# Selective scan on Trainium2: who adds the carried state, and how a product is cut between two engines

## The chip, the cores and the metric

The kernel runs on one core of one Trainium2 chip. The metric is the device time of one execution in microseconds (us); the time of the kernel before is the median of three runs. A core has five engines that run side by side, each with its own queue that is worked off in order: TensorE (PE, matrix products; its weight loads are shown as PEld), VectorE (DVE), ScalarE (ACT), GpSimd (POOL) and SyncE (SP), which here only starts DMA transfers. Engines wait for each other through semaphores. SBUF is the working memory of 128 partitions; PSUM is a smaller memory that TensorE writes to.

## The reference, cut to what matters

Four layers work on two images of 128 channels and 64 x 64 pixels: an attention layer, a layer of deformable convolutions, a residual convolution layer, and a selective scan ("Mamba") that reads each normalised image in four directions. Only the fourth is changed. Its core, for one direction of one image, with L = 4096 pixels, 256 inner channels and N = 16 states for each channel:

```python
dt = jax.nn.softplus(dt @ W_dt.T + b_dt)
A = -jnp.exp(A_log)
dA = jnp.exp(dt[..., None] * A)
dBu = dt[..., None] * Bm[:, :, None, :] * xh[..., None]

def step(h, inp):
    dA_t, dBu_t = inp
    h = dA_t * h + dBu_t
    return (h, h)
h0 = jnp.zeros((Bn, d_inner, N), x.dtype)
_, hs = lax.scan(step, h0, (dA.transpose(1, 0, 2, 3), dBu.transpose(1, 0, 2, 3)))
y = jnp.einsum('lbdn,bln->bld', hs, Cm)
```

So each of 256 x 16 sequences has a decay `dA`, an input `dBu` and a state `h` that runs through all 4096 pixels. The state starts from zero at the head of a direction.

## The kernel before, in words

The first three layers, which the change doesn't touch, fill the first 2450 us. The fourth, `layer3` (from L1121), has a short head and then, from about 2500 us to the end, one long loop (L1630).

**Tiling.** A direction is cut into 8 blocks of 512 pixels (`BLK`), so that two images of four directions make 64 blocks. In a block the 256 channels are two halves (`hf`) and the 16 states are four sets of four (`ng`): 8 groups `k`, in the order hf 0 with ng 0 to 3, then hf 1. A group covers 128 channels x 4 states; it is laid out as 4 scans (`q`, 32 channels each) of 128 partitions (4 states x 32 channels) and 512 columns. Every block therefore has 32 scans. Directions that run backwards read the same tiles from the last column to the first (`reverse`).

**What a group needs.** Six steps on four engines:

- *Input product* `dBu`, tile `db` (128 x 4 x 512): B times (dt times x), for all four scans. VectorE makes it in `db_dve` (L1413), with B spread over partitions by TensorE into a PSUM tile `pbc`; GpSimd makes it in `db_pool` (L1422), with B spread by DMA into an SBUF tile `b`. The table `ND` (L1130) says how many of the four scans are VectorE's: all four for five groups of a block, none for two (hf 0 ng 1 and hf 1 ng 2), and one of four for hf 0 ng 2, the mixed group.
- *Decay* `da` (128 x 512, PSUM): one exponential for each scan on ScalarE, `expo` (L1430).
- *Scan*: VectorE, `scan` (L1439), which runs h = da * h + db along the columns and overwrites `db`. Its start is the constant 0.0 in the first block of a direction, and else the column of `hl` that belongs to this group and scan.
- *Last state*: ScalarE, `keep` (L1444), which copies the last column of the group's four scans to `hl`, for the same group of the next block.
- *Product with C*: GpSimd, `cmul` (L1449), in place, after `keep`, since it overwrites the states.
- *Sum over states*: TensorE, `sums` (L1457).

**Order.** The loop writes the order of every engine's queue by hand (`manual_schedule`), group by group (k) and scan by scan (q). ScalarE makes decays two scans ahead (`AHEAD`), and the PSUM pool holds three `da` tiles, so that the decay of a scan waits until the scan three before it has ended. VectorE's product of group k+1 follows the last scan of group k; GpSimd's product of group k+2 follows `cmul(k-1)`. Between the groups, `front_act` gives ScalarE the next block's preparation: copies behind L1319's product (L1325, L1327), softplus, and two silu steps with table loads (L1300, L1313). In 13 of the 64 blocks the next image's normalisation runs as well (`ln_mean` to `ln_store`), one step to a slot.

The lines around the change:

```python
                for q in range(4):
                    ...
                    if 4 * k + q + AHEAD < len(units):
                        expo(*units[4 * k + q + AHEAD])
                    ...
                    if q == 0 and ended:
                        keep(k - 1)
                    if live:
                        scan(k, q)
```

Of the kernel before, what the change touches and what calls it, by code (L numbers as in the profile page):

```python
# [15 lines left out]
AF = mybir.ActivationFunctionType  # L16
ALU = mybir.AluOpType
# [3 lines left out]
P = 128  # L21
# [3 lines left out]
BLK = 512  # L25
NBLK = L // BLK
# [1094 lines left out]
def layer3(g, I, out):  # L1121
# [5 lines left out]
    nc, tc = g.nc, g.tc  # L1127
    NJ = 4

    ND = ((4, 0, 1, 4), (4, 4, 0, 4))  # L1130
    NNG = N_STATE // NJ
    HB = 1
    HC = 3
    with ExitStack() as ctx:
# [41 lines left out]
        d4 = ctx.enter_context(tc.tile_pool(name="l3d4", bufs=2))  # L1176
# [25 lines left out]
        hl = a.tile([P, 2, NNG, 4, 1], F32, name="hl")  # L1202
# [34 lines left out]
        def ln_log(b, k):  # L1237
            nc.scalar.activation(N[k, "sq"], N[k, "var"], AF.Ln, bias=g.eps5)
# [37 lines left out]
        def reverse(i):  # L1276
            b, nd, _ = blocks[i]
            return dirs[b][nd][2]

        S = {}  # L1280
# [113 lines left out]

        def copies(i, x, ng):

            if x == "b" and ND[0][ng] == ND[1][ng] == 4:
                return
            t = S[i][x, ng] = ck.tile([P, BLK], F32, name=f"{x}4_{ng}", bufs=1)
            r0 = NJ * ng + (N_STATE if x == "c" else 0)  # L1400
            for j in range(NJ):
                nc.sync.dma_start(t[32 * j : 32 * j + 32], S[i]["bx"][r0 + j].partition_broadcast(32))

        def db_tile(k):
            if "db" not in G[k]:
                G[k]["db"] = wk.tile([P, 4, BLK], F32, name="db")
            return G[k]["db"]

        def db_dve(k):
            i, hf, ng = groups[k]  # L1410
            n = ND[hf][ng]
            if n:
                nc.vector.tensor_tensor(  # L1413
                    db_tile(k)[:, :n, :], G[k].pop("pb").unsqueeze(1).to_broadcast([P, n, BLK]),
                    S[i]["d4", hf][:, 1, :n, :], ALU.mult,
                )

        def db_pool(k):
            i, hf, ng = groups[k]
            n = ND[hf][ng]  # L1420
            if n < 4:
                nc.gpsimd.tensor_tensor(  # L1422
                    db_tile(k)[:, n:, :], S[i]["b", ng].unsqueeze(1).to_broadcast([P, 4 - n, BLK]),
                    S[i]["d4", hf][:, 1, n:, :], ALU.mult,
                )

        def expo(k, q):
            i, hf, ng = groups[k]
            da = psd.tile([P, BLK], F32, name="da")
            nc.scalar.activation(da, S[i]["d4", hf][:, 0, q, :], AF.Exp, scale=am[:, hf, q, ng : ng + 1])  # L1430
            G[k]["da", q] = da

        def scan(k, q):
            i, hf, ng = groups[k]
            d0, d1 = G[k].pop(("da", q)), G[k]["db"][:, q, :]
            if reverse(i):
                d0, d1 = d0[:, ::-1], d1[:, ::-1]
            first = i % NBLK == 0
            nc.vector.tensor_tensor_scan(d1, d0, d1, 0.0 if first else hl[:, hf, ng, q, :], ALU.mult, ALU.add)  # L1439

        def keep(k):
            i, hf, ng = groups[k]
            last = 0 if reverse(i) else BLK - 1
            nc.scalar.copy(hl[:, hf, ng], G[k]["db"][:, :, last : last + 1])  # L1444
# [46 lines left out]
        G = {}  # L1491
# [75 lines left out]
        with tc.manual_schedule():  # L1567
            tc.keep_in_program_order(nc.scalar.preload_act_table_set("natural_log_exp_and_others"))
            nc.scalar.activation(am, am, AF.Exp)
            nc.vector.tensor_scalar(am, am, -1.0, None, ALU.mult)  # L1570
            nc.vector.memset(xt[:, :HC], 0.0)
            nc.vector.memset(xt[:, HC + L :], 0.0)
            nc.vector.memset(xn[:, HB - 1, HW - HC :], 0.0)
            nc.vector.memset(xn[:, HB + HW, :HC], 0.0)
            units = [(k, q) for k in range(len(groups)) for q in range(4)]
            AHEAD = 2

            for k in range(NFIRST):
                ln_mean(0, k)
            for k in range(NFIRST):  # L1580
                ln_less(0, k)
            ln_square(0, 0)
            ln_var(0, 0)
            ln_square(0, 1)
            ln_log(0, 0)
            ln_root(0, 0)
            ln_scale(0, 0)
            ln_var(0, 1)
            ln_square(0, 2)
            ln_store(0, 0)  # L1590
            ln_var(0, 2)
            begin(0)
            conv(0, 1)
            for part in (ln_log, ln_root, ln_scale):
                for k in (1, 2):
                    part(0, k)
            conv_silu(0)
            front_pe(0, 0)
            ln_store(0, 1)
            front_act(0, 0)  # L1600
            bc_store(0)
            front_pe(0, 1)
            front_act(0, 1)
            ln_store(0, 2)
            sum_parts(0, 0)
            sum_copy(0, 0)
            spread(0, 0)
            spread_store(0, 0)
            spread_load(0, 0)
            softplus(0, 1)  # L1610
            front_pe(0, 3)
            front_act(0, 3)
            spread(0, 1)
            spread_store(0, 1)
            for ng in range(NNG):
                copies(0, "b", ng)
                copies(0, "c", ng)
            for k in range(2):
                weights(k)
            db_dve(0)  # L1620
            db_pool(0)
            front_pe(0, 4)
            front_act(0, 4)
            front_pe(0, 5)
            front_pe(0, 6)
            for u in range(AHEAD):
                expo(*units[u])
            front_act(0, 7)
            db_pool(1)
            for k in range(len(groups) + 7):  # L1630
                i, slot = divmod(k, 8)
                live = k < len(groups)
                more = k + 1 < len(groups)
                ended = 1 <= k <= len(groups)
                transfers(i + 1, slot)
                if k + 2 < len(groups):
                    weights(k + 2)
                norm = next_norm(i)
                for q in range(4):
                    if slot == 6 and q == 3 and 1 <= i <= NBK:  # L1640
                        finish(i - 1)
                    if norm and slot == 2 and q == 3:
                        ln_log(*norm)
                    if 4 * k + q + AHEAD < len(units):
                        expo(*units[4 * k + q + AHEAD])
                    if norm and q == 0:
                        if slot == 0:
                            ln_mean(*norm)
                        elif slot == 2:
                            ln_var(*norm)  # L1650
                    if q == 0 and ended:
                        keep(k - 1)
                    if live:
                        scan(k, q)

                    for j, hf in (((k - 6) // 8, 0), ((k - 10) // 8, 1)):
                        if q == 1 and 8 * j + 6 + 4 * hf == k and 0 <= j < NBK:
                            gate(j, hf)
                if norm and slot == 0:
                    ln_less(*norm)  # L1660
                if more:
                    db_dve(k + 1)
                if ended:
                    cmul(k - 1)
                if k + 2 < len(groups):
                    db_pool(k + 2)

                if slot == 5 and 0 <= k - 2 < len(groups):
                    sums(k - 2)
                if slot == 5 and 1 <= i <= NBK:  # L1670
                    project(i - 1)
                front_pe(i + 1, slot)
                front_act(i + 1, slot)
                front_pool(i + 1, slot)
                if norm:
                    if slot == 1:
                        ln_square(*norm)
                    elif slot == 3:
                        ln_root(*norm)
                    elif slot == 5:  # L1680
                        ln_scale(*norm)
                    elif slot == 6:
                        ln_store(*norm)
                if live:

                    if slot == 6 and 0 < i % (4 * NBLK) <= NBLK // 2:
                        for n in range(2):
                            turn(blocks[i][0], 2 * (i % (4 * NBLK) - 1) + n)

                if slot != 5 and 0 <= k - 2 < len(groups):  # L1690
                    sums(k - 2)
# [160 lines left out]
```

## Time and profile before

| what | value |
|---|---|
| median of three runs | 5816.95 us (5814.35 to 5819.41) |
| the profiled execution's own time | 5815.21 us |
| its span in the profile | 5813.4 us |
| VectorE busy, whole span | 4427.0 us, 76% |
| GpSimd busy, whole span | 3620.8 us, 62% |
| ScalarE busy, whole span | 3827.3 us, 66% |
| 2500 to 5798 us (the scan loop): DVE, ACT, POOL busy | 3250.7, 2455.1, 3260.2 us of 3298 |
| mean granted TensorE clock | 0.889 |

How to read it: the profile is one execution, and every time in it counts from the first instruction. A group's row names the line, the engine, the operation, what it writes and reads, and the count; after the bar come its busy time in us and the mean length of one in ns, then the idle time of its engine just before such instructions, and who ended it. Records of one engine may overlap by some tens of ns[...]; so a run of equal instructions is read by the distance of their starts. In a list in order of time, neighbours of one kind are merged into a line: start, length of the whole, and `x4` for four of them.

### The profile page before, as it was taken

Reading aid. Unit: us, or ns where it says so; the run is one execution under the profiler, and the core shown is the slowest. Engines: PE = TensorE matmul, PEld = TensorE weight load, DVE = VectorE, ACT = ScalarE, POOL = GpSimd, SP = SyncE. Lnnn points to the kernel's source line nnn. Section 1 sums busy time; section 2 is a strip of 40 time slices with the busy share of each in tenths; the row PEclk is TensorE's granted clock in tenths of the full one; section 3 lists DMA queues with packets and bytes.
Section 4 is the critical chain, followed back from the end, with each engine's and each line's share of the span. In section 5 each row is a group of like instructions: output and inputs, shape, how many; then the busy total and the mean of one; then the engine's idle time right before and its main releaser. Section 6 shows DMA issues by size and latency. Waiting matters only on the chain.

```text
span 5813.4 us, 57554 instructions
## 1 busy us (share of the span) xinstructions
PE 4881.1 (84%) x19110; PEld 1732.0 (30%) x19110; DVE 4427.0 (76%) x4138; ACT 3827.3 (66%) x5499; POOL 3620.8 (62%) x1136
## 2 busy tenths in 40 slices
PE   7999999989978779977787777787788877777776
PEld 3333333334434334422222222222222222222221
DVE  5333333356124589779999999999999999999998
ACT  4888888850025521277777777777777777777775
POOL 5111111110010031179999999999999999999998
PEclk8999999999989889988888888888888888888886
DMA  5000001030046300065555555556655555555554
GB/s 157 19 19 19 19 19 33 1 60 1 1 90 121 74 18 0 6 143 128 135 130 131 143 140 129 128 130 148 145 129 136 127 134 143 139 129 135 132 139 102
DMA packets 333105, 541.88 MB, mean 93 GB/s; under 512 B 66384, under 2 KB 121184, under 8 KB 331712
## 3 DMA queue, kind: packets, MB, share of 16 engines
q1 hardware_dynamic: 329664, 534.58, 39.5%
q10 hardware_dynamic: 3136, 3.56, 0.2%
q8 instruction: 151, 2.47, 0.2%
q14 instruction: 154, 1.26, 0.1%
HBM read 448.81 MB, written 89.13 MB: 93 GB/s over the span
## 4 chain that ended last, share of the span: by engine, by line
DVE 50%; PE 37%; issue 4%; POOL 3%; DMA 3%; ACT 2%; SPq 1%; DVEq 0%; POOLq 0%; ACTq 0%
DVE db L1439 35%; DVE db L1413 11%; PE ps L287 11%; PE acc L303 9%; PE m L1052 6%; PE m L566 5%; PE acd L812 2%; DVE gt L1466 1%; PE m L526 1%; POOL db L1449 1%; POOL db L1422 1%; PE pf L775 1%; PE pc L663 1%; DMA c<-bx 1%; SPq L748 1%
## 5 line engine op out<-in xcount | busy, mean ns | idle before, releaser
L1449 POOL TENSOR_TENSOR db<-db,c 128x2048 f32<-128x2048 f32 x512 | 2310.8, 4532 | 36.5 <-ACT hl L1444 33.8
L1439 DVE TENSOR_TENSOR_SCAN db<-da,hl,db 128x512 f32<-128x512 f32 x1792 | 2154.7, 1263 | 40.4 <-ACT da L1430 3.5
L1430 ACT ACTIVATE da<-dd,am 128x512 f32<-128x512 f32 x2048 | 1402.2, 689 | 803.4 <-DVE db L1439 794.1
L293 ACT ACTIVATE e<-ps 128x1024 f16<-128x1024 f32 x1024 | 992.2, 1021 | 134.5 <-PE ps L287 117.2
L1422 POOL TENSOR_TENSOR db<-b,dd 128x2048 f32<-128x2048 f32 (+1 forms) x192 | 799.8, 4166 | 13.3 <-DMA b<-bx 13.3
L1457 PE MATMUL py<-db,fold 128*32 128x512 f32 x4096 | 618.0, 689 | 223.9 <-POOL db L1449 220.9
L1413 DVE TENSOR_TENSOR db<-pbc,dd 128x2048 f32<-128x2048 f32 (+1 forms) x384 | 766.5, 1996 | 32.0 <-DMA dd<-dx 32.0
L314 DVE RECIPROCAL rec<-acc 32x512 f32<-32x512 f32 x64 | 214.9, 3358 | 639.0 <-PE acc L303 612.1
L321 POOL TENSOR_TENSOR parts<-parts 32x512 f32<-32x512 f32 x64 | 80.4, 1257 | 975.1 <-DVE parts L320 975.1
L287 PE MATMUL ps<-q,k 32*128 32x512 f32 x4096 | 656.0, 643 | 3.5 <-DVE flag L250 2.7
L303 PE MATMUL acc<-e,v 128*128 128x512 f16 x2048 | 531.3, 382 | 0.0
L1052 PE MATMUL m<-v,u 128*128 128x512 f32 x864 | 376.1, 598 | 51.7 <-DVE v L1021 51.7
L1360 PE MATMUL pm<-dd,ident 128*128 128x512 f32 x512 | 356.6, 834 | 2.9 <-ACT dd L1353 2.7
L1392 PE MATMUL pbc<-bc,sel 64*128 64x512 f32 x384 | 207.5, 540 | 153.5 <-DVE db L1413 152.9
L1319 PE MATMUL pm<-u,wxp 128*72 128x512 f32 x256 | 189.4, 882 | 155.2 <-ACT u L1300 155.2
L303 PEld LDWEIGHTS <-v 128*128 128x128 bf16 x2048 | 158.5, 97 | 509.6 <-issue 388.3
L287 PEld LDWEIGHTS ps<-q,k 32*128 32x128 f32 x4096 | 229.7, 183 | 227.9 <-issue 146.2
L1439 DVE TENSOR_TENSOR_SCAN db<-da,db 128x512 f32<-128x512 f32 x256 | 292.3, 1202 | 6.2 <-ACT da L1430 1.3
L1457 PEld LDWEIGHTS py<-db,fold 128*32 128x32 f32 x4096 | 90.5, 114 | 607.0 <-POOL db L1449 356.4
L566 PE MATMUL m<-comb,w 64*128 64x512 f32 (+4 forms) x1296 | 269.9, 575 | 0.0
L1295 PE MATMUL pm<-xt,wcs 128*128 128x512 f32 x512 | 235.6, 602 | 24.6 <-ACT xa L1484 15.4
L686 POOL TENSOR_SCALAR yt<-y 32x512 f32<-32x512 f32 x8 | 18.2, 2271 | 381.7 <-DVE y L677 381.4
(318 smaller groups left out, 6031.8 us busy)
## 6 DMA issues: line engine op xcount, KB each, us to landing
dd<-dx SPq DMA_DIRECT2D x1024, 256.0 KB, 6.4
dx<-dd SPq DMA_DIRECT2D x128, 512.0 KB, 5.4
c<-bx SPq DMA_DIRECT2D x1024, 64.0 KB, 2.1
hats<-pos SPq DMA_DIRECT2D x136, 256.0 KB, 9.5
b<-bx SPq DMA_DIRECT2D x512, 64.0 KB, 4.5
q<-qd SPq DMA_DIRECT2D x32, 512.0 KB, 7.4
w<-in_conv0T SPq DMA_DIRECT2D x18, 288.0 KB, 8.6
q<-in_x SPq DMA_DIRECT2D x8, 512.0 KB, 7.2
```

What stands on the lines that cost most here:

```text
L287: nc.tensor.matmul(ps[:, i, :], k4[h % 2][rows, kb // 4, :], q4[h % 2][rows, qb * BLK : (qb + 1) * BLK], start=True, stop=True,)
L293: nc.scalar.activation(e[:, :n, :], ps[:, :n, :], AF.Exp)
L303: nc.tensor.matmul(acc, v3[b][:, kb, h, :], e[:, i, :], start=(kb == 0), stop=(kb == NS - 1))
L566: yield lambda q=q, dy=dy, src=src, i0=i0, i1=i1: nc.tensor.matmul(m[:, i0 * NF : i1 * NF], w[half, dy, q, x, :], src, start=(dy == KC and ...
L1052: nc.tensor.matmul(m[x], weights[j][:, dy, x, :], v[j][b][:, x, r0 : r0 + RP, :].rearrange("p r i -> p (r i)"), start=(dy == 0), stop=(dy ...
L1360: nc.tensor.matmul(ps, g.ident, S[i]["dd", hf][:, x, :], start=(x == 0), stop=(x == 1))
L1413: nc.vector.tensor_tensor(db_tile(k)[:, :n, :], G[k].pop("pb").unsqueeze(1).to_broadcast([P, n, BLK]), S[i]["d4", hf][:, 1, :n, :], ALU.mult,)
L1422: nc.gpsimd.tensor_tensor(db_tile(k)[:, n:, :], S[i]["b", ng].unsqueeze(1).to_broadcast([P, 4 - n, BLK]), S[i]["d4", hf][:, 1, n:, :], ALU ...
L1430: nc.scalar.activation(da, S[i]["d4", hf][:, 0, q, :], AF.Exp, scale=am[:, hf, q, ng : ng + 1])
L1439: nc.vector.tensor_tensor_scan(d1, d0, d1, 0.0 if first else hl[:, hf, ng, q, :], ALU.mult, ALU.add)
L1449: nc.gpsimd.tensor_mul(v, v, S[i]["c", ng].unsqueeze(1).to_broadcast([P, 4, BLK]))
L1457: nc.tensor.matmul(S[i]["y", hf][32 * q : 32 * q + 32, :], fold, G[k]["db"][:, q, :], start=False, stop=(ng == NNG - 1),)
```

## The change

Three edits, in `layer3` alone. The mixed group's product is cut by columns (176 of the 512 for VectorE, in all four scans) and not by scans. For 20 of a block's 32 scans, save in the first block of a direction, the scan starts from the constant 0.0; ScalarE adds the last state's share, decay of the first column times `hl`, to the first column of `db`, right after that scan's decay. These are scans 2 and 3 of every group, and scans 0 and 1 too of the two groups whose product is GpSimd's alone. And `keep` goes ahead of the decay in the same step of the loop.

```diff
-    ND = ((4, 0, 1, 4), (4, 4, 0, 4))
+    ND = ((BLK, 0, 176, BLK), (BLK, BLK, 0, BLK))
...
-            if x == "b" and ND[0][ng] == ND[1][ng] == 4:
+            if x == "b" and ND[0][ng] == ND[1][ng] == BLK:
...
-                    db_tile(k)[:, :n, :], G[k].pop("pb").unsqueeze(1).to_broadcast([P, n, BLK]),
-                    S[i]["d4", hf][:, 1, :n, :], ALU.mult,
+                    db_tile(k)[:, :, :n], G[k].pop("pb")[:, :n].unsqueeze(1).to_broadcast([P, 4, n]),
+                    S[i]["d4", hf][:, 1, :, :n], ALU.mult,
...
-            if n < 4:
+            if n < BLK:
                 nc.gpsimd.tensor_tensor(
-                    db_tile(k)[:, n:, :], S[i]["b", ng].unsqueeze(1).to_broadcast([P, 4 - n, BLK]),
-                    S[i]["d4", hf][:, 1, n:, :], ALU.mult,
+                    db_tile(k)[:, :, n:], S[i]["b", ng][:, n:].unsqueeze(1).to_broadcast([P, 4, BLK - n]),
+                    S[i]["d4", hf][:, 1, :, n:], ALU.mult,
                 )
+        def carried(k, q):
+            i, hf, ng = groups[k]
+            return i % NBLK > 0 and (q >= 2 or ND[hf][ng] == 0)
...
             nc.scalar.activation(da, S[i]["d4", hf][:, 0, q, :], AF.Exp, scale=am[:, hf, q, ng : ng + 1])
             G[k]["da", q] = da
+            if carried(k, q):
+                first = BLK - 1 if reverse(i) else 0
+                b0 = G[k]["db"][:, q, first : first + 1]
+                nc.scalar.activation(b0, da[:, first : first + 1], AF.Identity, bias=b0, scale=hl[:, hf, ng, q, :])
...
-            first = i % NBLK == 0
-            nc.vector.tensor_tensor_scan(d1, d0, d1, 0.0 if first else hl[:, hf, ng, q, :], ALU.mult, ALU.add)
+            zero = i % NBLK == 0 or carried(k, q)
+            nc.vector.tensor_tensor_scan(d1, d0, d1, 0.0 if zero else hl[:, hf, ng, q, :], ALU.mult, ALU.add)
...
+                    if q == 0 and ended:
+                        keep(k - 1)
                     if 4 * k + q + AHEAD < len(units):
                         expo(*units[4 * k + q + AHEAD])
...
-                    if q == 0 and ended:
-                        keep(k - 1)
                     if live:
                         scan(k, q)
```

In the changed kernel the addition is L1441, the scan L1449, `keep` L1454, `cmul` L1459 (so L1449 names GpSimd's product before and the scan after); the input products keep L1413 (VectorE) and L1422 (GpSimd).

## The prediction, on record ahead of the result

> **What bounds the kernel now.** I read the page first, then a table of busy time by windows, then the order of time on single engines. The page's chain of work that ended last gives VectorE half of the span, most of it the scan L1439, and these four groups carry the last layer:
>
> ```profile
> L1449 POOL TENSOR_TENSOR db<-db,c 128x2048 f32<-128x2048 f32 x512 | 2310.8, 4532 | 36.5 <-ACT hl L1444 33.8
> L1439 DVE TENSOR_TENSOR_SCAN db<-da,hl,db 128x512 f32<-128x512 f32 x1792 | 2154.7, 1263 | 40.4 <-ACT da L1430 3.5
> L1430 ACT ACTIVATE da<-dd,am 128x512 f32<-128x512 f32 x2048 | 1402.2, 689 | 803.4 <-DVE db L1439 794.1
> L1439 DVE TENSOR_TENSOR_SCAN db<-da,db 128x512 f32<-128x512 f32 x256 | 292.3, 1202 | 6.2 <-ACT da L1430 1.3
> ```
>
> VectorE scans and GpSimd products sit idle for only 40 and 36 us in all; ScalarE's exponentials wait 794 us for scans. So ScalarE follows, and it is between VectorE and GpSimd that the bound lies. The table by windows, one block of the scan to a window (busy time of PE, weight loads, DVE, ACT, POOL after the length), tells which:
>
> ```profile
> 4516.76:4568.30 51.54, 41.49 (x123) 12.69 (x122) 50.91 (x41) 38.20 (x63) 50.42 (x14) 0.82 0.56 135
> 4568.30:4617.92 49.62, 40.80 (x121) 12.88 (x121) 49.00 (x41) 37.94 (x63) 48.87 (x14) 0.82 0.58 139
> 4669.46:4721.00 51.54, 40.03 (x122) 12.38 (x121) 50.92 (x40) 38.16 (x63) 51.54 (x14) 0.86 0.56 133
> 3896.40:3949.40 53.00, 42.51 (x125) 13.35 (x125) 51.60 (x42) 40.29 (x67) 52.57 (x15) 0.83 0.56 136
> ```
>
> The second window is the first block of a direction, whose 32 scans start from the constant 0.0: it is 1.92 us shorter. An ordinary block keeps 51.54 us whether GpSimd is busy 50.42 or 51.54 us. VectorE sets that pace; GpSimd's need, averaged over a direction's eight blocks, is about 50.8 us, half a microsecond behind. The last window is a block that also normalises the next image; there VectorE loses about 0.8 us to a wait.
>
> VectorE's order in time shows that the 1.92 us is pace, not just a longer record:
>
> ```profile
> 3327.35 9.02 DVE L1439 TENSOR_TENSOR_SCAN db<-da,db 128x512 f32<-128x512 f32 x8
> 4617.91 9.51 DVE L1439 TENSOR_TENSOR_SCAN db<-da,hl,db 128x512 f32<-128x512 f32 x8
> ```
>
> Seven starts and one scan: (9.02 - 1.20)/7 = 1.117 us against (9.51 - 1.26)/7 = 1.179 us. A state read from `hl` costs a scan **0.061 us**; 32 x 0.061 = 1.95 agrees.
>
> ScalarE's order in time, at the head of an ordinary block (the third window above, from 4669.46), shows the narrow place:
>
> ```profile
> 4668.03 1.26 ACT L1300 ACTIVATE u<-pm,vecs 128x512 f32<-128x512 f32 x2
> 4669.31 1.28 ACT L1301 ACT_TABLE_LOAD   x1
> 4670.61 0.69 ACT L1430 ACTIVATE da<-dd,am 128x512 f32<-128x512 f32 x1
> 4671.24 0.18 ACT L1444 COPY hl<-db 128x4 f32<-128x4 f32 x1
> 4671.32 1.31 ACT L1430 ACTIVATE da<-dd,am 128x512 f32<-128x512 f32 x2
> 4673.12 0.69 ACT L1430 ACTIVATE da<-dd,am 128x512 f32<-128x512 f32 x1 [0.48 <-DVE db L1439]
> 4673.75 0.57 ACT L1325 COPY xd<-pm 72x512 f32<-72x512 f32 x1
> 4674.23 0.56 ACT L1327 CAST bc<-pm 32x512 fp32r<-32x512 f32 x1
> 4674.70 0.68 ACT L1430 ACTIVATE da<-dd,am 128x512 f32<-128x512 f32 x1
> ```
>
> After a silu and a table load, the decay for scan 2 of group 0 ends at 4671.30; that scan starts at 4671.83, two paces after the first (0.53 spare). The decay for scan 2 of group 1 ends at 4675.38; that scan starts at 4676.53 (1.15 spare), and 0.48 us of idle lies between.
>
> **What the skill says.** "ScalarE: Activation LUTs", Rules for kernel authors: about 0.3 us per ACTIVATE with a [128,1] bias, plus 0.83 ns an element. The trace agrees roughly: the one-column ACTIVATE `ga_sd` L84 took 262 ns, the four-column copy L1444 182 ns. "VectorE: DVE Perf Modes", the TRN2 errata section: an fp32 tensor_tensor is (N+151)/0.96 ns; the trace is slightly lower, 663 ns for 512 elements and 2263 for 2048 with one operand in PSUM. "SBUF — State Buffer", Who interferes with whom: a VectorE instruction with two SBUF inputs contends with GpSimd reads. Scan and product read one stream from PSUM, before and after; L1449 stays within 4490 to 4640 ns throughout, so no blocking is seen and none is added. No page I found prices a pointer start of a scan; the trace does.
>
> **The change, part by part.** An ordinary block has eight groups of four scans; `carried` takes q 2 and 3 of six groups and all four of the two groups that GpSimd multiplies: 20.
>
> *Scans.* 20 x 0.061 = -1.22 us a block on VectorE, 56 blocks; none in the eight first blocks.
>
> *Mixed product.* VectorE's part grows from 512 to 704 elements: 663 + 192 x (2263 - 663)/1536 = 863 ns, **+0.20 us** a block, all 64. GpSimd's falls from 1536 to 1344: between its rows (4527 and 3444) 2.12 ns an element, so 3.04 us, **-0.41**, leaving it about 50.4 us a block. Rows of 176 and 336 columns are not in the trace: bounds 3.0 (proportional) to 3.44 us (shorter rows eat the gain); I take 3.04. Scan 0 of this group now also waits for GpSimd, one scan earlier than scan 1 did. In a settled block GpSimd ended 0.23 us ahead of scan 0; it now starts about 0.6 us sooner (next item) and is 0.41 shorter, against scans 0.17 sooner: about 1 us spare. The unused-tile test in `copies` has the same outcome, so no DMA changes.
>
> *`keep` ahead of the decay.* The copy takes 0.09 us of issue (4671.24 to 4671.32), which the decay behind it now pays; GpSimd's L1449, waiting for the copy, comes up to 0.63 us sooner where ScalarE is late. It issues no DMA; past `ln_mean` and `ln_var` it moves in program order alone, as TensorE's order is unchanged.
>
> *The 20 additions.* Each waits for its decay (ScalarE's wait on itself: 0.03 us, seen before L1355), then runs. Duration: lower end 0.18 (L1444), upper 0.31 (skill); I take 0.262 (L84). Without overlap it occupies ScalarE about 0.03 + 0.26 = 0.29 us: 5.8 us a block, on 38.2 of 51.5. That total fits. It also waits for the product: for VectorE's, that ends before scan 0, where ScalarE would wait for a scan anyway; for GpSimd's, settled blocks have 3 us in hand. Behind a waiting addition queue the next decays, `keep` and the softplus and silu work, so scans wait next.
> At the narrow place, scan 2 of group 1 has five additions ahead of it. Budget: 1.15 + 0.48 idle - 0.09 (`keep`) - 0.30 (five scans sooner) = 1.24 us. Need: 5 x 0.29 = 1.45. **Stall 0.2 us a block** (from 0 at 0.21 us an addition to about 0.45 at 0.31). Scan 2 of group 0 needs 0.09 + 0.29 + 0.06 of 0.53 and fits.
>
> *Sum.* 45 ordinary blocks: 1.22 - 0.20 - 0.20 = 0.82 each, 36.9 us, giving 50.7 us a block, above GpSimd's 50.4. Eleven normalising blocks: their wait is at the same scan, behind L1325, so `keep` and that scan's own addition add 0.4 to 0.6 us; gain 0.4 each, 4.4. Eight first blocks: +0.20 each, +1.6. In all -39.7 against the profiled execution's own 5815.21 (span 5813.4 and 1.8 around it): 5775.5. That execution is 1.7 us under the median 5816.95, so **5777 us**.
>
> **Rivals.**
> *All of it fits.* Additions of 0.21 us or less; no stalls: 45 x 1.02 + 11 x 0.8 - 1.6 = 53, 5764 us. For it: 482 ns waits before most decays. Against: the sequence above.
> *GpSimd becomes the bound*, its mixed product keeping 3.44 us: 50.85 us for the 53 blocks without normalisation, against (45 x 51.55 + 8 x 49.62)/53 = 51.26: 22, plus 3: 5792 us. For it: half a microsecond of reserve. Against: both its forms fall on one line through element counts.
> *The gain goes into ScalarE's queue.* An addition of 0.40 us (longer for reading a column from PSUM with pointer scale and bias): stall 5 x 0.43 - 1.24 = 0.9; ordinary blocks gain 0.12, in all 8: 5809 us.
> *Slower.* The same place, group 1 scan 2, where five additions queue: from 0.42 us each (5 x 0.45 = 1.24 + 1.02) the stall exceeds what the scans save. At 0.50 us ordinary blocks lose 0.4: 17 + 1.6 - 3, 5833 us. Against: that is nearly twice L84.
> That the scans keep their 0.061 us is excluded by the first blocks, which run the same form.
>
> **How the numbers follow.** Forecast 0.57, all fits 0.13, GpSimd 0.12, queue 0.10, slower 0.08. Faster 0.82, same 0.10 (0.2%, 11.6 us, is about what a measurement of this kernel tells from no change), slower 0.08. Range: 5762, just under the case without stalls, to 5807, near the full-queue case; that holds the first three cases, 0.82.
>
> **What would show it.** 1120 scans should move from the `hl` form to the form without, at 1.117 us starts; L1441 should show 1120 entries near 262 ns; the mixed products 863 and 3040 ns; ordinary blocks 50.6 to 50.8 us; first blocks 49.8; and idle before scans put down to ScalarE, about 0.2 us a block. It would be wrong if L1441 is far from 262 ns, if the 336-column rows are dear, or if additions waiting for GpSimd hold up the decays behind them.

## The result, and the profile after

The changed kernel takes 5801.4 us (median of eight runs), the kernel before 5816.5 us beside it: a ratio of 0.9974, 95% interval 0.9965 to 0.9984. So it is faster, by 15 us, where the forecast was 40. The profiled execution took 5804.45 us, its span is 5802.7.

The page's groups, as before (ns of one after the busy time, then idle time and its end):

```profile
L1459 POOL TENSOR_TENSOR db<-db,c 128x2048 f32<-128x2048 f32 x512 | 2312.7, 4532 | 47.6 <-ACT hl L1454 33.3
L1449 DVE TENSOR_TENSOR_SCAN db<-da,db 128x512 f32<-128x512 f32 x1376 | 1585.0, 1203 | 35.4 <-ACT db L1441 28.5
L1435 ACT ACTIVATE da<-dd,am 128x512 f32<-128x512 f32 x2048 | 1398.1, 687 | 296.0 <-DVE db L1449 276.9
L1449 DVE TENSOR_TENSOR_SCAN db<-da,hl,db 128x512 f32<-128x512 f32 x672 | 825.9, 1271 | 40.6 <-POOL db L1422 3.5
L1441 ACT ACTIVATE db<-da,db,hl 128x1 f32<-128x1 f32 x1120 | 393.9, 352 | 148.4 <-DVE db L1413 104.0
```

1120 scans did move to the cheap form (256 + 1120 = 1376). But an addition takes 352 ns, not 262, and scans now sit idle for 28.5 us "<-ACT db L1441", a wait that did not exist before. ScalarE's own idle time ahead of decays fell from 803 to 296 us.

The table by windows, for a first block of a direction, an ordinary one and one that normalises (after the length: PE, weight loads, DVE, ACT, POOL):

```profile
4566.25:4616.11 49.86, 41.16 (x122) 12.90 (x121) 49.21 (x41) 37.97 (x63) 49.77 (x14) 0.82 0.59 138
4667.29:4718.47 51.18, 42.94 (x122) 13.10 (x121) 50.11 (x40) 43.83 (x83) 50.47 (x14) 0.80 0.55 134
3949.36:4002.42 53.06, 42.47 (x125) 13.29 (x125) 50.94 (x42) 46.23 (x87) 51.80 (x15) 0.83 0.57 136
```

The ordinary block is 51.18 us (51.54 before, 50.7 forecast). VectorE is busy for 50.11 of it (50.92 of 51.54 before), so that it now stands still for 1.07 us of the block, where it was 0.62; and GpSimd, busy 50.47, is not at work all the time either. Busy time alone doesn't say what holds the block up.

VectorE's order in time at the head of that ordinary block shows where it went:

```profile
4667.29 2.46 DVE L1449 TENSOR_TENSOR_SCAN db<-da,hl,db 128x512 f32<-128x512 f32 x2
4669.71 4.57 DVE L1449 TENSOR_TENSOR_SCAN db<-da,db 128x512 f32<-128x512 f32 x4
4674.68 2.34 DVE L1449 TENSOR_TENSOR_SCAN db<-da,db 128x512 f32<-128x512 f32 x2 [0.40 <-ACT db L1441]
4676.93 0.87 DVE L1413 TENSOR_TENSOR db<-pbc,dd 128x704 f32<-128x704 f32 x1
```

The hole of 0.40 us lies ahead of scan 2 of group 1, the place that the forecast named. ScalarE's order in the same microseconds:

```profile
4667.21 1.28 ACT L1301 ACT_TABLE_LOAD   x1
4668.50 0.20 ACT L1454 COPY hl<-db 128x4 f32<-128x4 f32 x1
4668.61 0.69 ACT L1435 ACTIVATE da<-dd,am 128x512 f32<-128x512 f32 x1
4669.33 0.35 ACT L1441 ACTIVATE db<-da,db,hl 128x1 f32<-128x1 f32 x1
4669.58 0.68 ACT L1435 ACTIVATE da<-dd,am 128x512 f32<-128x512 f32 x1
4670.29 0.35 ACT L1441 ACTIVATE db<-da,db,hl 128x1 f32<-128x1 f32 x1
...
4672.54 0.57 ACT L1325 COPY xd<-pm 72x512 f32<-72x512 f32 x1
4673.00 0.57 ACT L1327 CAST bc<-pm 32x512 fp32r<-32x512 f32 x1
4673.48 0.19 ACT L1454 COPY hl<-db 128x4 f32<-128x4 f32 x1
4673.58 0.68 ACT L1435 ACTIVATE da<-dd,am 128x512 f32<-128x512 f32 x1
4674.29 0.35 ACT L1441 ACTIVATE db<-da,db,hl 128x1 f32<-128x1 f32 x1
...
4675.51 1.29 ACT L1435 ACTIVATE da<-dd,am 128x512 f32<-128x512 f32 x2
```

Nothing here waits for VectorE any more: the queue runs without a hole of more than 0.1 us from the table load to the fifth addition, which ends at 4674.64; the scan starts 0.04 later. A decay followed by its addition takes 0.97 us to the next decay (4668.61 to 4669.58); two decays with nothing between them start about 0.62 apart (the last line: 1.29 for two of 0.68 that overlap). So an addition occupies ScalarE for about **0.345 us**, and five of them for 1.73, against the prediction's 1.24 us of room: 0.49 too much. The scan starts 1.596 us after the one before it, where the free pace is 1.114: 0.48.

### The profile page after: what moved, and what is told of

Same layout as the page of the kernel before. It is cut to its first block, busy times and chain, and to the rows that moved or that the text cites. A ratio compares the mean times of both kernels' runs of the same rounds, so it can differ in the third digit from the quotient of the medians.

```text
span 5802.7 us, 58641 instructions
## 1 busy us (share of the span) xinstructions
PE 4924.9 (85%) x19110; PEld 1750.9 (30%) x19110; DVE 4384.8 (76%) x4138; ACT 4150.5 (72%) x6619; POOL 3596.6 (62%) x1136
## 4 chain that ended last, share of the span: by engine, by line
DVE 42%; PE 38%; ACT 10%; issue 5%; POOL 2%; DMA 2%; SPq 1%; DVEq 0%; ACTq 0%; POOLq 0%
DVE db L1449 29%; PE ps L287 11%; DVE db L1413 10%; PE acc L303 9%; PE m L1052 6%; PE m L566 5%; ACT da L1435 3%; PE acd L812 2%; DVE gt L1476 1%; ACT db L1441 1%; PE m L526 1%; ACT u L1300 1%; ACT L1300 1%; PE pf L775 1%; SPq L748 1%
## 5 line engine op out<-in xcount | busy, mean ns | idle before, releaser
L1459 POOL TENSOR_TENSOR db<-db,c 128x2048 f32<-128x2048 f32 x512 | 2312.7, 4532 | 47.6 <-ACT hl L1454 33.3
L1449 DVE TENSOR_TENSOR_SCAN db<-da,db 128x512 f32<-128x512 f32 x1376 | 1585.0, 1203 | 35.4 <-ACT db L1441 28.5
L1449 DVE TENSOR_TENSOR_SCAN db<-da,hl,db 128x512 f32<-128x512 f32 x672 | 825.9, 1271 | 40.6 <-POOL db L1422 3.5
L1413 DVE TENSOR_TENSOR db<-pbc,dd 128x2048 f32<-128x2048 f32 (+1 forms) x384 | 781.0, 2034 | 31.7 <-DMA dd<-dx 31.7
L1422 POOL TENSOR_TENSOR db<-b,dd 128x2048 f32<-128x2048 f32 (+1 forms) x192 | 773.0, 4026 | 12.6 <-DMA b<-bx 12.6
L1441 ACT ACTIVATE db<-da,db,hl 128x1 f32<-128x1 f32 x1120 | 393.9, 352 | 148.4 <-DVE db L1413 104.0
```

Source lines behind the costliest of these rows:

```text
L1413: nc.vector.tensor_tensor(db_tile(k)[:, :, :n], G[k].pop("pb")[:, :n].unsqueeze(1).to_broadcast([P, 4, n]), S[i]["d4", hf][:, 1, :, :n], A ...
L1422: nc.gpsimd.tensor_tensor(db_tile(k)[:, :, n:], S[i]["b", ng][:, n:].unsqueeze(1).to_broadcast([P, 4, BLK - n]), S[i]["d4", hf][:, 1, :, n ...
L1441: nc.scalar.activation(b0, da[:, first : first + 1], AF.Identity, bias=b0, scale=hl[:, hf, ng, q, :])
L1449: nc.vector.tensor_tensor_scan(d1, d0, d1, 0.0 if zero else hl[:, hf, ng, q, :], ALU.mult, ALU.add)
L1459: nc.gpsimd.tensor_mul(v, v, S[i]["c", ng].unsqueeze(1).to_broadcast([P, 4, BLK]))
```

## The experiments

The theory, Q: VectorE still sets the pace of an ordinary block, and the queue on ScalarE ahead of scan 2 of group 1 (five additions of 0.345 us) took much of the gain back. Its rivals: L, the additions cost by their total load on ScalarE, wherever they stand; G, GpSimd is the bound at about 51 us; and later K, GpSimd is what the earlier copy protects. Times of ordinary, first and normalising blocks below run from the start of a block's first scan to that of the next block, from the traces; ordinary is a median. Groups and scans are counted from 0. Every run was timed beside the kernel before (medians of 5817.5 to 5818.1 us).

**1. Two additions fewer where the queue is tight**

```diff
-            return i % NBLK > 0 and (q >= 2 or ND[hf][ng] == 0)
+            return i % NBLK > 0 and (q >= 2 or ND[hf][ng] == 0) and not (k % 8 == 1 and q < 2)
```

> The changed kernel without two of its 20 additions: scans 0 and 1 of group 1 start from the stored state again. Theory Q (the queue on ScalarE ahead of scan 2 of group 1 is what ate the gain: five additions of 0.345 us of occupancy each against 1.24 us of room): two fewer take 0.69 us from that queue, the stall of 0.48 us goes, two scans cost 0.061 us more each; an ordinary block falls from 51.18 to about 50.8 us, the kernel from 5801 to about 5783 us. Rival L (ScalarE's load in all, 20 additions a block, slows the block wherever they stand): two of twenty are a tenth, 5799 to 5802 us. Rival G (GpSimd is the bound at about 51.0 us a block): no change, 5801 us.

Measured: 5786.9 us, ratio to before 0.9949 (0.9935 to 0.9962); ordinary blocks 50.79 us. VectorE's order in time at the head of an ordinary block:

```profile
4650.27 2.46 DVE L1449 TENSOR_TENSOR_SCAN db<-da,hl,db 128x512 f32<-128x512 f32 x2
4652.69 2.34 DVE L1449 TENSOR_TENSOR_SCAN db<-da,db 128x512 f32<-128x512 f32 x2
4654.94 2.43 DVE L1449 TENSOR_TENSOR_SCAN db<-da,hl,db 128x512 f32<-128x512 f32 x2
4657.29 2.31 DVE L1449 TENSOR_TENSOR_SCAN db<-da,db 128x512 f32<-128x512 f32 x2
```

The hole is gone. Taking two additions away brings 14.5 us, although two scans in each ordinary block became dearer. G, which expected no change, is out; L, which expected 2 us at most, waits for the control.

**2. The control: two fewer where there is room**

```diff
-            return i % NBLK > 0 and (q >= 2 or ND[hf][ng] == 0)
+            return i % NBLK > 0 and (q >= 2 or ND[hf][ng] == 0) and not (k % 8 == 4 and q >= 2)
```

> The control: two additions are dropped as well, but those of scans 2 and 3 of group 4, where the changed kernel has over 1.4 us in hand. Theory Q: the stall of 0.48 us stays, two scans cost 0.061 us more each; ordinary blocks 51.30 us, 5801 plus 56 x 0.12 = about 5808 us. Rival L: the same as dropping them at group 1, 5799 to 5802 us. Rival G: 5801 us.

Measured: 5806.2 us, ratio 0.9982 (0.9975 to 0.9989); ordinary blocks 51.30 us, the 0.12 more of two dearer scans. Waits of scans for L1441 stay at 28.1 us. The total alone can't be told from that of the changed kernel, as the intervals overlap; the sign is read from the blocks. The same number of additions dropped, and ordinary blocks 0.12 us longer, where experiment 1 made them 0.39 shorter: place decides, not load.

**3. One addition fewer**

```diff
-            return i % NBLK > 0 and (q >= 2 or ND[hf][ng] == 0)
+            return i % NBLK > 0 and (q >= 2 or ND[hf][ng] == 0) and not (k % 8 == 1 and q == 0)
```

> The changed kernel without one addition, that of scan 0 of group 1. Theory Q, by its sum: four additions, 4 x 0.345 - 1.24 = 0.14 us of stall in place of 0.48, and 0.06 us more for one scan: ordinary blocks 50.90 us, between the changed kernel's 51.18 and 50.79 with two dropped; about 5789 us. A theory in which these two additions wait for GpSimd's product, and hold up the queue by that wait, expects nothing from dropping one, since the other waits in its place: 51.2 us, 5804 us.

Measured: 5785.4 us, ratio 0.9946 (0.9932 to 0.9959); ordinary blocks 50.81 us. One is nearly enough, more than the sum expected (50.90): it had left out that the scan without its addition is 0.06 us slower and so gives the queue that much more room. With it, 4 x 0.345 - 1.24 - 0.06 = 0.08 of lateness; by the distances of starts, scan 2 of group 1 was 0.06 late and scan 3 a further 0.03. That the two additions wait for GpSimd's product does not fit: one dropped was nearly enough, and in the changed kernel additions wait for L1422 only twice, 1.6 us in all.

**4. The two tight places freed**

```diff
-            return i % NBLK > 0 and (q >= 2 or ND[hf][ng] == 0)
+            return i % NBLK > 0 and (q >= 2 or ND[hf][ng] == 0) and not (k % 8 in (0, 1) and q == 2)
```

> The changed kernel without the additions of scan 2 in groups 0 and 1, the two places where its scans waited for ScalarE. Theory Q: scan 2 of group 1 has three additions ahead of it, 3 x 0.345 = 1.04 of 1.24 us, so its stall of 0.48 us goes; the 0.07 us at group 0 goes; two scans cost 0.061 each: ordinary blocks 50.75 us. In normalising blocks, where L1325 waits for TensorE just ahead, only this scan's own addition counts, so they gain up to 0.3 us, which the drop at scans 0 and 1 of group 1 could not give. In all about 5778 us. Rival L (load in all): two of twenty, 5799 to 5802 us. Rival G: 5801 us.

Measured: 5778.0 us, ratio 0.9935 (0.9921 to 0.9948), so its interval lies under that of the changed kernel; ordinary blocks 50.72 us; normalising ones 52.49 on average (52.66 before, 52.83 in the changed kernel). The list of waits in the scan loop, in the changed kernel (who waited for whom: us in total, times, longest):

```profile
POOL db L1459 <- ACT hl L1454: 33.3, 46, 2.6
DVE db L1449 <- ACT db L1441: 28.5, 56, 1.4
```

and in this one:

```profile
POOL db L1459 <- ACT hl L1454: 19.1, 34, 2.7
DVE db L1449 <- POOL db L1422: 6.9, 8, 1.3
```

Scans now wait for an addition once, 0.3 us. For GpSimd's product they wait 6.9 us (3.5 in the changed kernel), in six normalising blocks and two ordinary ones; experiment 8 comes back to it.

**5. What an addition costs, by its operands**

```diff
-                nc.scalar.activation(b0, da[:, first : first + 1], AF.Identity, bias=b0, scale=hl[:, hf, ng, q, :])
+                h0, d0 = hl[:, hf, ng, q, :], da[:, first : first + 1]
+                if k % 8 == 1:
+                    nc.scalar.activation(b0, h0, AF.Identity, bias=b0, scale=h0)
+                elif k % 8 == 6:
+                    nc.scalar.copy(b0, d0)
+                elif q == 2:
+                    nc.scalar.activation(b0, d0, AF.Identity, bias=b0)
+                else:
+                    nc.scalar.activation(b0, d0, AF.Identity, scale=h0)
```

> A measurement of the addition by its operands; what is added to the first column is changed, so its output is not the reference's. Scan 2 has the bias as a pointer and no scale, scan 3 the scale as a pointer and no bias, group 1 both pointers with the source in SBUF in place of PSUM, group 6 a plain copy from PSUM. If each pointer operand costs the same, the forms step from about 175 ns (copy) by 90 to about 262 ns (one pointer) and 352 (two). If what costs is that bias and output are one column, the bias form alone is 350 and the scale form 260 or less. If the source's place counts, the SBUF form differs from 352.

What is added is no longer the right value here; this run only measures times. A pointer is an operand that the instruction reads from a [128,1] column. One column each; the groups by form, in the order bias only, scale only, both with the source in SBUF, plain copy:

```profile
L1447 ACT ACTIVATE db<-da,db 128x1 f32<-128x1 f32 x336 | 87.9, 261 | 112.0 <-DVE db L1413 102.2 <-ACT da L1435 0.2
L1449 ACT ACTIVATE db<-da,hl 128x1 f32<-128x1 f32 x336 | 87.8, 261 | 10.9
L1443 ACT ACTIVATE db<-hl,db 128x1 f32<-128x1 f32 x224 | 83.5, 373 | 1.3 <-POOL db L1422 1.1
L1445 ACT COPY db<-da 128x1 f32<-128x1 f32 x224 | 35.7, 159 | 10.5 <-ACT da L1435 0.4
```

The time steps with the pointers: 159, 261, 352 ns for none, one and two, and bias and scale count alike. The step from one to two, 91 ns, is the second pointer's price; the first step also changes the operation, from COPY to ACTIVATE. That bias and output are one column costs nothing. A source in SBUF adds 21 ns.

This run also shows what shorter additions do to the queue. Its queue to scan 2 of group 1 holds two of the one-pointer form, which occupy 0.25 us each (0.876 us from decay to next decay), and three of the SBUF form, 0.265 each although they last 373 ns: they read no decay, so they start before the decay ahead of them has ended. That is 1.30 us in all, where the forecast had 1.45 and the changed kernel 1.73, and ordinary blocks took 50.71 us: with all 20 additions in place the lateness of scan 2 of group 1 shrinks from 0.48 to 0.09 us. (One profiled execution, 5780.6 us.)

**6. The column cut without additions**

```diff
-            return i % NBLK > 0 and (q >= 2 or ND[hf][ng] == 0)
+            return False
```

> Two of the three edits alone: the column cut and the earlier copy of last states, with no additions and every scan starting from the stored state. Theory Q: VectorE sets the pace, so the column cut costs its 0.24 us a block and the earlier copy brings nothing; ordinary blocks 51.83 us, about 5816.5 + 64 x 0.25 = 5832 us. Rival G: GpSimd has 0.41 us less to do in a block and is the bound, so this is faster than before, by up to 26 us.

Measured: 5831.5 us, ratio 1.0026 (1.0016 to 1.0036); ordinary blocks 51.79 us. The cut by columns and the earlier copy together are a loss of 14 us by themselves; the gain comes from the additions.

**7. The cut by scans with additions**

```diff
-    ND = ((BLK, 0, 176, BLK), (BLK, BLK, 0, BLK))
+    ND = ((4, 0, 1, 4), (4, 4, 0, 4))
...
-                    db_tile(k)[:, :, :n], G[k].pop("pb")[:, :n].unsqueeze(1).to_broadcast([P, 4, n]),
+                    db_tile(k)[:, :n, :], G[k].pop("pb").unsqueeze(1).to_broadcast([P, n, BLK]),
```

(and GpSimd's half likewise)

> The changed kernel with the mixed product cut by scans again (VectorE one scan of four, GpSimd three); additions and earlier copy stay. Theory Q: VectorE loses 0.24 us of work, GpSimd gains 0.41 and needs about 50.8 us a block; ordinary blocks 50.9 to 51.0 us, in all 5790 to 5796 us. Rival G: 0.41 us more on the bound, 64 x 0.41 = 26 us slower than the changed kernel, 5827 us.

Measured: 5789.6 us, ratio 0.9953 (0.9940 to 0.9967); ordinary blocks 50.95 us, with the 0.40 us hole still there, and normalising ones 52.55. In the changed kernel the column cut costs 0.23 us a block and buys nothing, because there the hole, and not GpSimd, is what scans wait for.

**8. The same cut with the tight places freed**

The edits of 4 and 7 together.

> The version without the two tight additions (scan 2 of groups 0 and 1), with the mixed product cut by scans again, so that GpSimd has 0.43 us a block more and VectorE 0.23 less. Theory Q: VectorE would take 50.72 - 0.23 = 50.49 us for an ordinary block, but GpSimd needs about 50.8 to 50.9, so that GpSimd becomes the bound and ordinary blocks take 50.8 to 50.9 us, with waits for L1422 or for GpSimd's share of db in them; about 5780 us. Rival V (VectorE sets every block, GpSimd's half microsecond never matters): 50.49 us and about 5766 us.

Measured: 5782.8 us, ratio 0.9942 (0.9928 to 0.9955). An ordinary block of experiment 4 in the table by windows, and one of this run:

```profile
4651.43:4702.15 50.72, 42.96 (x123) 13.06 (x122) 50.05 (x40) 43.26 (x81) 50.72 (x14) 0.80 0.58 135
4699.26:4750.05 50.79, 39.91 (x123) 12.05 (x122) 49.95 (x41) 43.26 (x81) 50.79 (x14) 0.87 0.57 135
```

GpSimd is busy throughout in both, as in some blocks of the kernel before, so its busy time doesn't tell whether it is the bound. The waits of scans do, here:

```profile
DVE db L1449 <- POOL db L1422: 10.8, 28, 0.9
```

In 42 of the 45 ordinary blocks, the first scan that needs GpSimd's mixed product (scan 1 of group 2) starts within 0.04 us of the product's end, and in the median 0.28 us behind its pace; in experiment 4 the first scan that needs the product (there scan 0) starts 1.16 us after its end, in the median. Ordinary blocks took 50.79 us, where V expected 50.49: once the hole is closed, GpSimd is the bound unless the column cut relieves it. That decides against V.

**9. The tight places freed, 160 columns for VectorE**

```diff
-    ND = ((BLK, 0, 176, BLK), (BLK, BLK, 0, BLK))
+    ND = ((BLK, 0, 160, BLK), (BLK, BLK, 0, BLK))
```

with the edit of 4.

> The version without the two tight additions, with VectorE's part of the mixed product at 160 columns in place of 176. Theory Q: VectorE 0.067 us less a block, GpSimd 0.136 more, 50.6 against 50.65, both below 50.72: ordinary blocks 50.65 us, about 5775 us, 0 to 4 us faster than 5778; where GpSimd's waits grow in normalising blocks this may vanish. Rival V: 50.65 us too, and no growth in normalising blocks.

Measured: 5777.2 us, ratio 0.9931 (0.9917 to 0.9944); ordinary blocks 50.64 us. It can't be told from 4 by its total, and since both theories expected 50.65 us for ordinary blocks, it doesn't test them there; normalising blocks did not grow (52.46 us against 52.49), which Q had left open and V expected. Both versions beat the kernel before and the changed one.

**10. The copy of last states behind the decay**

```diff
-                    if q == 0 and ended:
-                        keep(k - 1)
                     if 4 * k + q + AHEAD < len(units):
                         expo(*units[4 * k + q + AHEAD])
+                    if q == 0 and ended:
+                        keep(k - 1)
```

> The changed kernel with the copy of last states behind the decay and its addition again. Theory Q: the copy's 0.09 to 0.10 us leave the queue ahead of scan 2 of group 1 and of group 0; ordinary blocks 51.08 us, about 5796 us, as GpSimd, whose products then start up to 1.07 us later, has that in hand in ordinary blocks. Rival K: GpSimd's later start becomes the wait that ends last, and the kernel is slower than the changed one by up to 64 x 0.6 = 38 us, 5840 us.

Measured: 5807.8 us, ratio 0.9984 (0.9977 to 0.9990). Ordinary blocks are 51.08 us, as Q had it; but first blocks rose from 49.86 to 50.17 us and normalising ones by 0.3, with waits for GpSimd's product:

```profile
DVE db L1449 <- ACT db L1441: 27.7, 59, 1.2
DVE db L1449 <- POOL db L1422: 14.8, 21, 1.1
```

So Q missed the total by 12 us, and K holds in part: the earlier copy keeps GpSimd out of the way in first and normalising blocks. The loss against the changed kernel is read from these blocks and not from the totals, whose intervals overlap. The additions alone, with neither of the other two edits, were not run.

## Why the prediction was half right

Direction, bound and place were right; the size was not. By its own steps, in the two profiled executions:

| step | forecast | measured |
|---|---|---|
| scans, ordinary block | -1.22 us | 20 starts 0.061 shorter, -1.22 |
| mixed product on VectorE | +0.20 | +0.235 (start to next start 0.766, now 1.001) |
| GpSimd's mixed product | 3.04 us | 3.03 |
| an addition, its length | 0.262 us | 0.352 |
| an addition, what it occupies of ScalarE | 0.29 us | 0.345 |
| stall at scan 2 of group 1 | +0.20 | +0.48, and 0.03 as its next scan restarts |
| scan 2 of group 0 | fits | +0.07 |
| 45 ordinary blocks | -36.9 | -16.6 |
| 11 normalising blocks | -4.4 | +1.9 |
| 8 first blocks | +1.6 | +1.6 (seven longer by 0.24 to 0.36, one shorter by 0.22: partly luck) |

- **The step that failed is the price of an addition**: "Duration: lower end 0.18 (L1444), upper 0.31 (skill); I take 0.262 (L84)". All three have at most one pointer operand; the addition has two, and experiment 5 shows 0.09 us for the second. The true 0.352 us lay outside the stated bounds, and the stall was more than twice its forecast. The forecast's own formula with the measured 0.345 us of occupancy, 5 x 0.345 - 1.24 = 0.48, gives the measured stall; experiments 1 and 3 follow it with two and one addition fewer. In 45 blocks, (0.28 + 0.03 at group 1 + 0.07 at group 0) x 45 = 17 of the 20 us that the ordinary blocks fell short; the other 3 are products (the mixed one 0.035, the five whole ones 0.008 each).
- **That the formula meets the stall to the hundredth is luck.** Its 0.30 us for "five scans sooner" has one scan too many, as four shorter ones stand ahead of that scan in its block, 0.24 us; and the table load that opens the queue ended 1.20 us after the block's first scan began, where it had been 1.14. These two cancel. In all, scan 2 of group 1 starts 0.55 us behind the free pace, of which 0.07 stem from group 0, so the formula is good to somewhat under 0.1 us.
- **The rival "The gain goes into ScalarE's queue"** had this mechanism, with an addition of 0.40 us for its two pointers and 5809 us. The kernel lies between it and the forecast.
- **Normalising blocks** were mis-sized too. Their scan 2 of group 1 does wait longer, as the prediction put it: in the eleven blocks VectorE stands still there for 10.6 us, against 3.5 before, 0.64 a block and so a little over the forecast's 0.4 to 0.6. Two things were not forecast: scan 2 of group 3 starts 0.17 us late in every one of them, and in two the first scan of the mixed group waited about 1 us for GpSimd. The prediction counted GpSimd's spare time for "a settled block" and did not work it out for these, where GpSimd has 1.27 us more to do. With the addition freed (4) they took 52.49 us: the first wait fell to 4.4 us, but that for GpSimd grew to 4.7. With the cut by scans as well (8) they took 52.24.
- **GpSimd as the bound** did not happen in ordinary blocks, as its product fell with the element count; 8 shows that the half microsecond of reserve was the right thing to watch.
- **"All of it fits"** (5764 us) is what 4 and 5 come near: 5778 and 5781 us.
- The two profiled executions differ by 3.6 us before the first scan (2500.8 and 2504.4 us), in layers that the change doesn't touch; in the other traces that head ended between 2496.0 and 2504.8. That is noise of the same size as the smaller terms, and it accounts for most of why the two profiles differ by 10.7 us where the medians differ by 15.

## What to carry to other kernels

When work moves to an engine with idle time, look for its longest stretch without a wait, add up what is new in that stretch alone, and compare it with the slack at its end; the engine's mean load did not tell it here (experiments 1 and 2). Price a tiny instruction by a row of a profile with the same number of pointer operands, or give the bound room for each operand that no row has. Tell a bound by who waits for whom, not by busy time: GpSimd was busy throughout in blocks that it held up and in blocks that it did not (experiment 8). And where one item in a tight stretch costs more than it saves, drop that item alone: 18 additions beat 20.

## What the runs showed of the hardware

- A scan of 512 columns that starts from a [128,1] column and not from a constant takes 0.061 us more from start to start; in the median ordinary block this showed at every position that moved, save next to the two waits.
- A one-column instruction on ScalarE took 159 ns as a copy, 261 as an ACTIVATE with one pointer, 352 with two.
- What it occupies is not its length. The 352 ns addition that reads the decay just ahead starts after that decay's end and occupies 0.345 us; the 373 ns one that doesn't read it starts before that end and occupies 0.265.
